# A two-layer graph kernel: attention and scores of the last batches as one block of matmuls, with bank copies and statistics moved

## Chip, cores and metric

The kernel runs on one core of a Trainium2 chip. The metric is device time in microseconds (us), the median of several runs; lower is better. Engines are named as in the profile: PE (TensorE), DVE (VectorE), ACT (ScalarE), POOL (GpSimd), and SP, which issues the DMAs.

## What is computed

There are 128 batches of a 128 x 512 matrix `x` in fp32, and one 128 x 128 matrix `adj`, which is a weight in layer 0 and the attention mask in layer 1.

```python
def layer0(x, W1, W2, b):                 # W1 = W2 = adj
    A = einsum('od,bdn->bon', W1, x)
    C = einsum('od,bdn->bon', W2, x) + b[None, :, None]
    pre = A[:, :, None, :] + (C - A)[:, :, :, None]
    return max(relu(pre), axis=-1)

def layer1(x, w_qkv, w_proj, b_proj, gamma, beta, mask):   # H = 8 heads of 64
    q, k, v = split_heads(x @ w_qkv)
    attn = einsum('bhnd,bhmd->bhnm', q, k) * scale
    attn = softmax(where(mask == 0, -inf, attn))
    o = merge_heads(attn @ v) @ w_proj + b_proj
    return o + layernorm(o) * gamma + beta

x = layernorm(x + layer0(x, adj, adj, L0_gnn_b))
x = layernorm(x + layer1(x, w_qkv, w_proj, b_proj, gamma, beta, adj))
```

Since both weights of layer 0 are the same matrix, its result is one number per row, `max(A) + b`, cut at zero.

## The kernel before

**Tiling.** Batches go through in 32 groups of four (`G = 4`). The projections of a group (queries and keys in two units, values, output) are computed with a seven-product scheme: a `Unit` stands for a matrix of 2 x 2 blocks made from seven products instead of eight. Each `product(i)` is four matmuls of 128x128 by 128x256, which the profile lists as eight, and adds into one of four PSUM banks, b1 to b4: products 1, 6 and 7 into bank 1, product 2 into bank 2, products 5 and 3 into bank 3, product 4 into bank 4. The left sides are the four blocks and four sums of blocks (s1 to s4, called `s_x` and `s_o` in the profile). Products 5, 6 and 7 use the first, second and third sum, product 3 the fourth.

**Copies of bank 1.** After product 1 (`snap(1)`), product 6 (`snap(2)`) and product 7 (`snap(3)`) ACT copies bank 1 to SBUF. `result(half, col)` on DVE adds such a copy to another bank. A product into bank 1 has to wait until the copy before it has read the bank. `relay()` copies bank 1 into bank 2 instead, so that product 2 adds onto it, and `relayed()` copies bank 2 to its place: two copies on ACT instead of a copy on ACT and a sum on DVE. `seed(unit, bank)` writes the bias into a bank before the first product into it.

**Attention.** `scores(b, banks)` makes eight small matmuls (64 rows deep) into two banks, `softmax_mask` scales and masks them on DVE, `softmax_max` takes the maxima on DVE, `softmax_exp` is eight exponentials on ACT, `prob_out` divides and transposes on DVE and writes to DRAM through SP, `prob_read` reads back, `attend` makes eight small matmuls (64 columns wide) into one bank, and `attend_copy` copies this on ACT.

**Tails.** `tail_inner` (ACT) applies the layer norm to a projected output, `tail_residual` (POOL, three steps: gamma, output, residual rows) finishes the sum, `tail_outer` (ACT) is the last norm, and a store follows. `stats` takes means and variances on DVE (`bn_stats`, `bn_aggr`) and finishes them on POOL: an addition, a power, and, for entries that are normalized on ACT, a product. With `fused=1` the first entry is normalized on DVE and leaves this product out. `fused_open`, `fused_close` (DVE) and `add_rows` (PE) do a tail in another way, `scalar_stats` takes statistics on ACT.

**Order.** Every instruction is pinned: each engine runs its own instructions in the order in which the program lists them, SP's DMAs too. A head (first eight batches of layer 0), a loop over pairs of batches, and a last part, with `L = 127` (the last batch), `LQ = 63` (the last pair) and `NG = 32`, are written out by hand. In the loop, `group_block` puts the attends of four batches and the scores of the next four directly behind each other on PE. In the last part the attends of batches 120 and 121 and the scores of 124/125 and 126/127 stand apart, with products between them. `keep_warm` multiplies zeros in the head.

[...] A new tile in a bank waits for the readers of the old one.

Of the kernel before, what the change touches and what calls it, by code (L numbers as in the profile page):

```python
# [16 lines left out]
def kernel(  # L17
# [33 lines left out]
    H = 8  # L51
    HD = D // H
    KC = D // P
    G = 4
# [250 lines left out]
    def l0_norm(f):  # L305
        normalize(xs[f], xs[f], ("y", f))

    def l0_norm_vector(f, mv):
        rs, _ = stat_of.pop(("y", f))
        pin(nc.vector.tensor_scalar(xs[f], xs[f], mv[:, 0, 0:1], rs, ALU.subtract, ALU.mult))  # L310
# [91 lines left out]
    def scores(b, banks=("pss0", "pss1")):  # L402
        g, h, jj = place(b)
        pss[b] = [
            psum.tile([P, NP, P], F32, tag=tag, name=f"pss{par}_{b}")
            for par, tag in enumerate(banks)
        ]
        for pr in range(NP):
            for par in range(2):
                t = qk[g, pr // 2, h][ds(par * HD, HD), :, pr % 2, ts(jj, P)]  # L410
                pe(pss[b][par][:, pr], lhsT=t[:, 0], rhs=t[:, 1], start=True, stop=True)

    def softmax_mask(b, order=(0, 1), place=None):

        s = place or sb.tile([P, 2, NP, P], F32, tag="s", name=f"s_{b}", bufs=4)
        for par in order:
            pin(
                nc.vector.scalar_tensor_tensor(  # L418
                    s[:, par],
                    pss[b][par],  # L420
                    SCALE,
                    mask.unsqueeze(1).to_broadcast([P, NP, P]),
                    ALU.mult,
                    ALU.add,
                )
            )
        del pss[b]
        prob[b] = s.rearrange("p a h m -> p (a h) m")

    def softmax_max(b):  # L430
        if b in pss:
            softmax_mask(b)
        nmax[b] = small.tile([P, H], F32, tag="nmax", name=f"nmax_{b}")
        pin(nc.vector.tensor_reduce(nmax[b], prob[b], AX.X, ALU.max, negate=True))  # L434

    def softmax_exp(b, heads=range(H)):
        if 0 in heads:
            psums[b] = small.tile([P, H], F32, tag="sums", name=f"sums_{b}")
        for i in heads:
            pin(  # L440
                nc.scalar.activation(  # L441
                    prob[b][:, i],
                    prob[b][:, i],
                    AF.Exp,
                    bias=nmax[b][:, i : i + 1],
                    accum_out=psums[b][:, i : i + 1],
                )
            )
# [44 lines left out]
    def attend(b, tag="po"):  # L493
        g, h, jj = place(b)
        v, t = vs[g, h], pT.pop(b)
        pos[b] = psum.tile([P, NP, P], F32, tag=tag, name=f"po_{b}")
        for pr in range(NP):
            for par in range(2):
                pe(
                    pos[b][ds(par * HD, HD), pr],  # L500
                    lhsT=v[:, jj, ds((2 * pr + par) * HD, HD)],
                    rhs=t[:, :, par * NP + pr],
                    start=True,
                    stop=True,
                )

    def attend_copy(b):
        g, h, jj = place(b)
        if jj == 0:
            tag = "x" if (g, h) == (NG - 2, 0) else "oT"  # L510
            oT[g, h] = sb.tile([P, KC, HT], F32, tag=tag, name=f"oT_{g}_{h}", bufs=2)
        pin(nc.scalar.copy(oT[g, h][:, :, ts(jj, P)], pos.pop(b)))
# [88 lines left out]
    def tail_inner(q):  # L601
        zp[q] = sb.tile([P, 2, D], F32, tag="z", name=f"z_{q}")
        for j in range(2):
            b = 2 * q + j
            normalize(zp[q][:, j], o_of(b), ("o", b))
            zs[b] = rs_[b]

    def tail_residual(q):
        z, r, (g, h) = zp.pop(q), xr.pop(q), divmod(q, 2)
        rs_pair[q] = r  # L610
        tt(nc.gpsimd, z, z, ga_bc.unsqueeze(1).to_broadcast([P, 2, D]), ALU.mult)
        tt(nc.gpsimd, z, z, os_[g, h], ALU.add)
        tt(nc.gpsimd, r, r, z, ALU.add)
# [27 lines left out]
    def tail_inner_one(b):  # L641
        z_tile(b)
        normalize(zs[b], o_of(b), ("o", b))
# [31 lines left out]
    def columns(name, *items):  # L675

        mv = small.tile([P, NC, 2], F32, tag="mv", name=f"mv_{name}")
        for k, (kind, b) in reversed(list(enumerate(items))):
            bn({"o": o_of, "z": zs.get, "y": xs.get}[kind](b), mv, k)
        return mv, items  # L680

    def stats(name, *items, fused=0):
        stat = columns(name, *items)
        finish_stats(*stat, fused)
        return stat[0]
# [40 lines left out]
        l0_add(f)  # L726
    stats("first_0", ("y", 0))
    l0_norm(0)
    mv = stats("first_1", ("y", 1), fused=1)
    weight_sums(wqk, 0, HE, 1)  # L730
    l0_max(2)
    l0_add(2)
    l0_norm_vector(1, mv)
    keep_warm(3)
    for f in range(2):
        l0_transpose_pe(f)
    l0_max(3)
    l0_add(3)
    weight_sums(wqk, 0, HE, 2)
    mv = stats("first_2", ("y", 2), ("y", 3), fused=1)  # L740
    l0_norm_vector(2, mv)
    l0_norm(3)
    weight_sums(wqk, 0, HE, 3)
    weight_sums(wqk, HE, HE)
    keep_warm(2)
# [7 lines left out]
    cur.snap(1)  # L753
    cur.product(2)
    l0_mm(4, "pa")
    for f in range(2, G):
        l0_transpose_pe(f)
    for f, tag in zip(range(5, 2 * G), ("po", "pss0", "pss1")):
        l0_mm(f, tag)
    run_sums(sums[:3], nc.vector)  # L760
    run_sums(sums[3:])
# [2 lines left out]
        l0_spill(q)  # L764
    cur.result(0, 0)
    cur.product(4)
    cur.product(5)
    cur.product(6)
    cur.snap(2)
    for f in range(G, 2 * G):  # L770
        l0_max(f)
        if f < 2 * G - 1:
            l0_add(f)
# [319 lines left out]
    second.snap(2)  # L1093
    second.product(5)
    second.result(0, 0)
    second.product(4)
    second.product(7)


    before, o_u, v_u = second, o_unit(NG - 3), v_unit(NG - 1)  # L1100
    attend(L - 7)
    before.snap(3)
    seed(o_u, 1)
    attend_copy(L - 7)
    attend(L - 6, "pa")
    attend_copy(L - 6)
    before.result(1, 1)
    before.result(1, 0)
    prob_out(L - 4)
# [3 lines left out]
    o_u.relay()  # L1113
    tail_outer(LQ - 7)
    tail_store(LQ - 7)
    tail_inner(LQ - 6)
    before.product(3)
    before.result(0, 1)
    seed(o_u, 3)
    tail_residual(LQ - 6)  # L1120
    o_u.product(2)
    o_u.relayed()
    scores(L - 3)
    scores(L - 2, po_pa)
    tail_reload(LQ - 5)
    wlast, room = last_load()
    for q in range(3):
        tail_reload_to(LQ - 2 + q, room[:, ds(2 * q, 2)])
    softmax_max(L - 3)
    softmax_max(L - 2)  # L1130
    place_of = {
        b: room[:, ds(2 * q, 2)].rearrange("p a (h m) -> p a h m", m=P)
        for b, q in ((L - 1, 3), (L, 4))
    }
    o_u.product(6)
    o_u.snap(2)
    softmax_exp(L - 3)
    o_u.product(4)
    o_u.product(5)
    o_u.product(7)  # L1140
    scores(L - 1)
    scores(L, po_pa)
    softmax_exp(L - 2, range(4))
    o_u.snap(3)
    softmax_exp(L - 2, range(4, H))
    prob_out(L - 3)
    o_u.result(1, 1)
    o_u.result(1, 0)
    softmax_mask(L - 1, place=place_of[L - 1])
    softmax_max(L - 1)  # L1150
    stats("last_1", ("o", L - 9), ("o", L - 8))
    v_u.product(1)
    v_u.relay()
    softmax_exp(L - 1, range(4))
    o_u.product(3)
    v_u.product(2)
    o_u.result(0, 1)
    prob_out(L - 2)
    softmax_exp(L - 1, range(4, H))
    v_u.relayed()  # L1160
    softmax_mask(L, place=place_of[L])
    softmax_max(L)
    for t in (L - 9, L - 8):
        tail_inner_one(t)
        tail_residual_one(t)
    v_u.product(6)
    v_u.snap(2)
    softmax_exp(L)
    v_u.product(5)
    v_u.product(7)  # L1170
    v_u.snap(3)
    v_u.product(4)
    stat = columns("last_2", ("o", L - 11), ("o", L - 10))
    prob_out(L - 1)


    o_u = o_unit(NG - 2)
    seed(o_u, 1)
    attend(L - 5)
    attend_copy(L - 5)  # L1180
    attend(L - 4, "pa")
    attend_copy(L - 4)
    prob_read(L - 3)
    prob_read(L - 2)
    v_u.result(1, 1)
    v_u.result(1, 0)
    run_sums(o_sums(NG - 2))
    o_u.lefts = o_lefts[NG - 2]
    o_u.product(1)
# [5 lines left out]
    o_u.product(2)  # L1195
    o_u.relayed()
    seed(o_u, 3)
    for t in (L - 11, L - 10):
        tail_inner_one(t)
    o_u.product(4)  # L1200
    o_u.product(6)
    o_u.snap(2)
    last_seed(L - 3, "b2")
    tail_residual_one(L - 11)
    stats("last_3", ("z", L - 13), ("z", L - 12), ("z", L - 9), ("z", L - 8))
# [51 lines left out]
    fused_close(L - 3)  # L1257
    tail_residual_one(L - 4, [0, 1])
    tail_outer_one(L - 7)
    mv = stats("last_8", ("o", L - 1), ("z", L - 6), ("z", L - 3), fused=1)  # L1260
    fused_open(L - 1, mv[:, 0, 0:1], rows=False)
    add_rows(L - 1)
    fused_close(L - 2)
    finish_scalar_stats(stat5)
    tail_residual_one(L - 4, [2])
    for t in (L - 3, L - 6, L - 5):
        tail_outer_one(t)
    stat4 = scalar_stats(L - 4)
    mv = stats("last_9", ("o", L), ("z", L - 2), fused=1)
    fused_open(L, mv[:, 0, 0:1], rows=False)  # L1270
    add_rows(L)
    fused_close(L - 1)
    tail_outer_one(L - 2)
    stats("last_10", ("z", L - 1))
    finish_scalar_stats(stat4)
    fused_close(L)
    for t in (L - 1, L - 4):
        tail_outer_one(t)
    mv = stats("last_11", ("z", L), fused=1)
    tail_outer_vector(L, mv[:, 0, 0:1])  # L1280


# [39 lines left out]
```

## Time and profile before

| | |
|---|---|
| median of 3 runs | 1933.93 us (1933.15 to 1934.26) |
| the profiled execution | 1933.73 us, its span 1931.9 us |
| busy in the span | PE 1918.5, DVE 1592.1, POOL 1290.4, ACT 1054.2 us |
| granted PE clock | 0.999 |
| head: PE's first product | starts at 14.43 us |
| last part: products of the unit `second` | start at 1841.18 us |
| last matmul on PE | starts at 1923.39 us |
| last tile finished on DVE | 1928.92 us |

The span runs from the first to the last instruction; the 1.8 us between it and the time of the same execution lie around it. "Busy" of PE includes matmuls that overlap, so that start-to-start distances are the better price of a matmul. The profile also names for each engine what ended its waits. All moments below are us from the start of the span.

### The profile page before, as it was taken

The page shows a single profiled execution, that of the slowest core. Times are in us where ns is not written, and L with a number is a line of the kernel's source. Part 1 is how long each engine was busy: PE and PEld are TensorE (multiplying, and loading weights), DVE is VectorE, ACT ScalarE, POOL GpSimd, SP SyncE. Part 2 cuts the span into 40 slices and gives each one's busy share as a digit, 9 for nine tenths or more (in the row PEclk, how much of TensorE's full clock was granted, in tenths as well). Part 3 has the DMA queues.
Part 4 walks back from the last instruction along what each step waited for, and adds up shares of the span by engine and source line. Part 5 has one row for each costly group of instructions (what it writes and reads, how often), then busy time and mean ns, then how long its engine had stood idle before and what let it go on. Part 6 is the DMA issues. An engine that isn't in the chain of part 4 may idle for free.

```text
span 1931.9 us, 33367 instructions
## 1 busy us (share of the span) xinstructions
PE 1918.5 (99%) x11541; PEld 1638.3 (85%) x11541; DVE 1592.1 (82%) x2514; ACT 1054.2 (55%) x3093; POOL 1290.4 (67%) x823
## 2 busy tenths in 40 slices
PE   9999999999999999999999999999999999999997
PEld 6888888888888888888888888888888888888885
DVE  6867888888888888888888888888888888888887
ACT  3444655645555556555465564555555555556476
POOL 6445766767667676676676676866767666667648
PEclk9999999999999999999999999999999999999999
DMA  7756676676676666766666756667666676666665
GB/s 221 175 134 152 172 189 176 171 183 159 186 202 159 186 161 180 205 161 177 171 176 188 182 167 186 153 186 207 154 186 164 183 200 164 175 178 172 164 209 162
DMA packets 444936, 341.76 MB, mean 177 GB/s; under 512 B 276832, under 2 KB 378336, under 8 KB 444768
## 3 DMA queue, kind: packets, MB, share of 16 engines
q1 hardware_dynamic: 444336, 338.85, 65.7%
q8 instruction: 91, 1.49, 0.3%
q10 hardware_dynamic: 432, 0.79, 0.1%
q14 instruction: 77, 0.63, 0.1%
HBM read 172.82 MB, written 166.72 MB: 176 GB/s over the span
## 4 chain that ended last, share of the span: by engine, by line
PE 96%; DVE 2%; POOL 1%; ACT 1%; issue 0%; POOLq 0%; ACTq 0%; DVEq 0%
PE b_qk L75 40%; PE b_v L75 19%; PE b_o L75 19%; PE pss L75 6%; PE po L75 6%; PE pa L75 6%; DVE st_mv_last L262 0%; POOL zl L78 0%; POOL s_o L78 0%; ACT s L441 0%; DVE s L78 0%; PE idle L75 0%; DVE o L78 0%; DVE mv_last L263 0%; DVE pu L462 0%
## 5 line engine op out<-in xcount | busy, mean ns | idle before, releaser
L75 PE MATMUL b_qk<-s_x,wqk 128*128 128x256 f32 x2048 | 473.1, 379 | 0.7 <-ACT u_qk L187 0.7
L75 PEld LDWEIGHTS b_qk<-s_x,wqk 128*128 128x128 f32 x2048 | 389.0, 190 | 54.5 <-ACT u_qk L187 1.1
L441 ACT ACTIVATE s<-s,nmax 128x128 f32<-128x128 f32 x1008 | 390.2, 391 | 4.5 <-DVE nmax L434 4.5
L75 PE MATMUL b_qk<-x1T,wqk 128*128 128x256 f32 x1536 | 360.5, 381 | 0.1
L276 POOL TENSOR_SCALAR rs_mv<-mv 128x6 f32<-128x6 f32 (+2 forms) x61 | 14.8, 243 | 499.9 <-DVE mv L263 499.9
L75 PEld LDWEIGHTS b_qk<-x1T,wqk 128*128 128x128 f32 x1536 | 289.3, 190 | 43.0 <-issue 1.0
L78 DVE TENSOR_TENSOR s<-s,rec 128x1024 f32<-128x1024 f32 x126 | 282.2, 2240 | 4.3
L78 DVE TENSOR_TENSOR qk<-b_qk,u_qk 128x512 f32<-128x512 f32 x256 | 170.2, 686 | 138.8 <-ACT u_qk L187 86.5
L187 ACT COPY u_qk<-b_qk 128x512 f32<-128x512 f32 x192 | 112.5, 586 | 278.2 <-PE b_qk L75 276.7
L75 PE MATMUL b_v<-wv,s_x 128*128 128x256 f32 x1024 | 237.2, 379 | 0.2
L75 PE MATMUL b_o<-wp,s_o 128*128 128x256 f32 x992 | 229.6, 379 | 0.4 <-ACT u_o L187 0.4
L418 DVE SCALAR_TENSOR_TENSOR s<-pss,mask 128x512 f32<-128x512 f32 x252 | 156.2, 681 | 78.1 <-PE pss L75 77.9
L75 PEld LDWEIGHTS b_v<-wv,s_x 128*128 128x128 f32 x1024 | 194.3, 190 | 27.4 <-DVE qk L78 0.5
L75 PEld LDWEIGHTS b_o<-wp,s_o 128*128 128x128 f32 x992 | 188.2, 190 | 26.5 <-issue 0.9
L78 POOL TENSOR_TENSOR z<-z,ga_bc 128x1024 f32<-128x1024 f32 x58 | 164.0, 2827 | 51.1 <-ACT z L285 51.1
L441 ACT ACTIVATION_READ_ACCUMULATOR s<-s,nmax 128x1 f32 x1008 | 190.8, 189 | 0.0
L78 POOL TENSOR_TENSOR x<-x,be_bc 128x1024 f32<-128x1024 f32 x64 | 178.2, 2785 | 17.5 <-DVE xt L323 16.2
L187 ACT COPY u_v<-b_v 128x512 f32<-128x512 f32 x95 | 55.6, 585 | 244.6 <-PE b_v L75 241.7
L187 ACT COPY u_o<-b_o 128x512 f32<-128x512 f32 x91 | 53.3, 586 | 248.0 <-PE b_o L75 248.0
L75 PE MATMUL b_v<-wv,x1T 128*128 128x256 f32 x768 | 176.5, 379 | 0.0
L75 PEld LDWEIGHTS b_v<-wv,x1T 128*128 128x128 f32 x768 | 145.8, 190 | 32.3 <-issue 13.9
L75 PE MATMUL b_o<-wp,oT 128*128 128x256 f32 x744 | 171.1, 379 | 0.3 <-ACT b_o L556 0.3
(135 smaller groups left out, 3309.8 us busy)
## 6 DMA issues: line engine op xcount, KB each, us to landing
hop<-pu SPq DMA_DIRECT2D x128, 512.0 KB, 3.1
pT<-hop SPq DMA_DIRECT2D x512, 128.0 KB, 3.6
spill<-x SPq DMA_DIRECT2D x64, 512.0 KB, 5.0
x<-in_x_dram SPq DMA_DIRECT2D x62, 512.0 KB, 4.3
xhop<-xt SPq DMA_DIRECT2D x248, 128.0 KB, 2.3
x1T<-xhop SPq DMA_DIRECT2D x248, 128.0 KB, 3.9
xr<-spill SPq DMA_DIRECT2D x59, 512.0 KB, 3.4
out_dram<-xr SPq DMA_DIRECT2D x58, 512.0 KB, 4.2
```

The costliest lines, as they stand in the source:

```text
L75: pin(nc.tensor.matmul(*args, **kwargs))
L78: pin(eng.tensor_tensor(dst, a, b, op))
L187: pin(nc.scalar.copy(t, self.banks[1]))
L276: pin(nc.gpsimd.tensor_scalar(rs[:, :n], mv[:, :n, 1], EPS, None, ALU.add))
L418: nc.vector.scalar_tensor_tensor(s[:, par], pss[b][par], SCALE, mask.unsqueeze(1).to_broadcast([P, NP, P]), ALU.mult, ALU.add,)
L441: nc.scalar.activation(prob[b][:, i], prob[b][:, i], AF.Exp, bias=nmax[b][:, i : i + 1], accum_out=psums[b][:, i : i + 1],)
```

## The change

In the head, batch 1 is normalized on ACT instead of DVE; of batches 2 and 3, batch 2's statistics come first on DVE, 3 is normalized on DVE and 2 on ACT, and they are transposed in the order 3, 2. In the first unit product 5 moves behind product 6 and its copy.

In the last part, product 7 of the unit `second` and its copy move ahead of product 4. The attends of batches 120 and 121 move from the front of the next stage into one block with the scores of batches 124 to 127, which use other banks (the fourth takes those of the first again); the masks follow the block in a given order. The tail of batches 114 and 115 (`LQ - 6`) and the reloads with `last_load` move behind the block. The exponentials of batches 124 to 127 are divided anew between the copies of bank 1. `v_u.relay()` and `v_u.relayed()` become `v_u.snap(1)` and `v_u.result(0, 0)`. `o_unit(NG - 2)` and its seed move ahead of the last twelve exponentials, and `v_u.result(1, 1)` and `(1, 0)` ahead of the last attends. `tail_inner_one` of batches 116 and 117 moves behind product 6 of the next unit. At the very end, statistics, outer norms and the third residual step of batch 123 change places, each of batches 125, 126 and 127 has statistics of its own, and the last norm of batch 126 goes to DVE.

```diff
     stats("first_0", ("y", 0))
     l0_norm(0)
-    mv = stats("first_1", ("y", 1), fused=1)
+    stats("first_1", ("y", 1))
+    l0_norm(1)
     weight_sums(wqk, 0, HE, 1)
     l0_max(2)
     l0_add(2)
-    l0_norm_vector(1, mv)
...
-    mv = stats("first_2", ("y", 2), ("y", 3), fused=1)
-    l0_norm_vector(2, mv)
-    l0_norm(3)
+    mv = stats("first_2", ("y", 3), ("y", 2), fused=1)
+    l0_norm_vector(3, mv)
+    l0_norm(2)
...
-    for f in range(2, G):
+    for f in (3, 2):
         l0_transpose_pe(f)
-    for f, tag in zip(range(5, 2 * G), ("po", "pss0", "pss1")):
+    for f, tag in zip(range(5, 2 * G), ("po", "pss1", "pss0")):
         l0_mm(f, tag)
...
     cur.product(4)
-    cur.product(5)
     cur.product(6)
     cur.snap(2)
+    cur.product(5)
...
     second.product(5)
     second.result(0, 0)
+    second.product(7)
+    second.snap(3)
     second.product(4)
-    second.product(7)
...
     before, o_u, v_u = second, o_unit(NG - 3), v_unit(NG - 1)
-    attend(L - 7)
-    before.snap(3)
     seed(o_u, 1)
-    attend_copy(L - 7)
-    attend(L - 6, "pa")
-    attend_copy(L - 6)
     before.result(1, 1)
...
-    tail_inner(LQ - 6)
     before.product(3)
     before.result(0, 1)
     seed(o_u, 3)
-    tail_residual(LQ - 6)
     o_u.product(2)
     o_u.relayed()
-    scores(L - 3)
-    scores(L - 2, po_pa)
+    for t, tag in zip((L - 7, L - 6), po_pa):
+        attend(t, tag)
+        attend_copy(t)
+    for t, banks in zip(
+        range(L - 3, L + 1), (("pss0", "pss1"), ("po", "b4"), ("pa", "b2"), ("pss0", "pss1"))
+    ):
+        scores(t, banks)
+    tail_inner(LQ - 6)
+    tail_residual(LQ - 6)
     tail_reload(LQ - 5)
     wlast, room = last_load()
...
-    softmax_max(L - 3)
-    softmax_max(L - 2)
...
+    softmax_mask(L - 3)
+    softmax_mask(L - 2, (1, 0))
+    softmax_max(L - 3)
+    softmax_mask(L - 1, (1, 0), place_of[L - 1])
+    softmax_mask(L, place=place_of[L])
+    softmax_max(L - 2)
     o_u.product(6)
     o_u.snap(2)
-    softmax_exp(L - 3)
-    o_u.product(4)
+    softmax_exp(L - 3, range(4))
     o_u.product(5)
     o_u.product(7)
-    scores(L - 1)
-    scores(L, po_pa)
-    softmax_exp(L - 2, range(4))
     o_u.snap(3)
-    softmax_exp(L - 2, range(4, H))
+    softmax_exp(L - 3, range(4, H))
+    o_u.result(1, 1)
+    o_u.product(4)
+    o_u.result(1, 0)
+    v_u.product(1)
+    v_u.snap(1)
+    o_u.product(3)
+    softmax_exp(L - 2)
     prob_out(L - 3)
-    o_u.result(1, 1)
-    o_u.result(1, 0)
-    softmax_mask(L - 1, place=place_of[L - 1])
+    o_u.result(0, 1)
+    v_u.product(2)
+    v_u.result(0, 0)
     softmax_max(L - 1)
     stats("last_1", ("o", L - 9), ("o", L - 8))
-    v_u.product(1)
-    v_u.relay()
+    v_u.product(6)
+    v_u.snap(2)
     softmax_exp(L - 1, range(4))
-    o_u.product(3)
-    v_u.product(2)
-    o_u.result(0, 1)
     prob_out(L - 2)
-    softmax_exp(L - 1, range(4, H))
-    v_u.relayed()
-    softmax_mask(L, place=place_of[L])
     softmax_max(L)
     for t in (L - 9, L - 8):
         tail_inner_one(t)
         tail_residual_one(t)
-    v_u.product(6)
-    v_u.snap(2)
-    softmax_exp(L)
     v_u.product(5)
     v_u.product(7)
     v_u.snap(3)
+    o_u = o_unit(NG - 2)
+    seed(o_u, 1)
+    softmax_exp(L - 1, range(4, H))
+    softmax_exp(L)
     v_u.product(4)
+    v_u.result(1, 1)
+    v_u.result(1, 0)
     stat = columns("last_2", ("o", L - 11), ("o", L - 10))
     prob_out(L - 1)
-    o_u = o_unit(NG - 2)
-    seed(o_u, 1)
...
-    v_u.result(1, 1)
-    v_u.result(1, 0)
...
     seed(o_u, 3)
-    for t in (L - 11, L - 10):
-        tail_inner_one(t)
     o_u.product(4)
     o_u.product(6)
     o_u.snap(2)
+    for t in (L - 11, L - 10):
+        tail_inner_one(t)
...
     tail_outer_one(L - 7)
+    finish_scalar_stats(stat5)
+    tail_outer_one(L - 5)
     mv = stats("last_8", ("o", L - 1), ("z", L - 6), ("z", L - 3), fused=1)
...
     fused_close(L - 2)
-    finish_scalar_stats(stat5)
-    tail_residual_one(L - 4, [2])
-    for t in (L - 3, L - 6, L - 5):
+    for t in (L - 3, L - 6):
         tail_outer_one(t)
-    stat4 = scalar_stats(L - 4)
-    mv = stats("last_9", ("o", L), ("z", L - 2), fused=1)
+    mv = stats("last_9", ("o", L), fused=1)
     fused_open(L, mv[:, 0, 0:1], rows=False)
     add_rows(L)
     fused_close(L - 1)
+    tail_residual_one(L - 4, [2])
+    stat4 = scalar_stats(L - 4)
+    stats("last_10", ("z", L - 2))
     tail_outer_one(L - 2)
-    stats("last_10", ("z", L - 1))
+    fused_close(L)
+    mv = stats("last_11", ("z", L), fused=1)
     finish_scalar_stats(stat4)
-    fused_close(L)
-    for t in (L - 1, L - 4):
-        tail_outer_one(t)
-    mv = stats("last_11", ("z", L), fused=1)
+    tail_outer_one(L - 4)
+    mv1 = stats("last_12", ("z", L - 1), fused=1)
     tail_outer_vector(L, mv[:, 0, 0:1])
+    tail_outer_vector(L - 1, mv1[:, 0, 0:1])
```

## The prediction

> **What bounds the kernel now.** I read four views. The page first: PE is busy 1918.5 of 1931.9 us, and the chain that ended last is nearly all PE.
>
> ```profile
> PE 96%; DVE 2%; POOL 1%; ACT 1%; issue 0%; POOLq 0%; ACTq 0%; DVEq 0%
> ```
>
> So only PE's own time counts up to about 1900, and PE's waits (second view: us in total, times, longest) say what was lost:
>
> ```profile
> PE pp L75 <- DVE z L654: 1.5, 1, 1.5
> PE pt L333 <- DVE x L310: 0.7, 2, 0.4
> PE b_qk L75 <- ACT u_qk L187: 0.7, 1, 0.7
> PE b_o L75 <- ACT u_o L187: 0.4, 1, 0.4
> PE b_o L75 <- ACT b_o L556: 0.3, 1, 0.3
> ```
>
> The third view, PE's timeline of the last part, gives prices (start, duration):
>
> ```profile
> 1767.13 3.84 PE L75 MATMUL pss<-qk 64*128 64x128 f32 x64
> 1770.90 1.99 PE L75 MATMUL b_qk<-x1T,wqk 128*128 128x256 f32 x8
> ...
> 1853.45 1.97 PE L75 MATMUL po<-pT,v 128*64 128x128 f32 x32
> 1855.35 1.99 PE L75 MATMUL b_o<-wp,oT 128*128 128x256 f32 x8
> ...
> 1860.72 2.06 PE L75 MATMUL pss<-qk 64*128 64x128 f32 x32
> 1862.71 1.99 PE L75 MATMUL b_o<-wp,s_o 128*128 128x256 f32 x8
> ...
> 1869.81 2.06 PE L75 MATMUL pss<-qk 64*128 64x128 f32 x32
> ```
>
> A product (8 matmuls) is 1.73 from start to start and 1.83 after another kind of matmul. Past 1900, DVE is dense in the chain and POOL nearly so. The fourth view, the timelines of ACT, DVE and POOL, shows what the moved steps wait for:
>
> ```profile
> 1849.97 0.57 ACT L187 COPY u_qk<-b_qk 128x512 f32<-128x512 f32 x1
> ...
> 1885.42 0.56 ACT L187 COPY u_v<-b_v 128x512 f32<-128x512 f32 x1
> 1886.02 0.59 ACT L556 COPY b_o<-bp_bc 128x512 f32<-128x512 f32 x1
> ```
>
> ```profile
> 1889.64 2.14 POOL L78 TENSOR_TENSOR s_o<-s_o,oT 128x512 f32<-128x512 f32 x1
> 1891.74 1.27 POOL L78 TENSOR_TENSOR s_o<-oT,oT 128x512 f32<-128x512 f32 x1
> ```
>
> [...] v_u.product(7) ended at 1882.5, but its copy (snap 3) began at 1885.42, behind eight exponentials that ended at 1885.33, and cost PE 0.33. [...] The trace shows it as the 0.7 wait for u_qk: product 7 writes bank 1 and waits until snap 2 has read it. [...] the POOL sum at 1889.64 takes 2.14 instead of 1.27 beside the DVE division of 1888.53, itself 2.12 instead of 1.23.
>
> **Part 1, the head.** Normalizing batch 1 on DVE took 1.48 (11.31 to 12.80). On ACT it needs one more POOL multiply (0.2, after the power ended at 11.28) and 0.81: done at 12.4, 0.4 earlier. This passes through transposes, DVE copies and l0_max(3) to l0_add(3), which ends at 15.5 instead of 15.9. Statistics of batch 2 now precede those of batch 3 and fill DVE's wait for l0_add(3); only batch 3's remain behind it, 0.79 less. From its aggregate (16.4 instead of 17.6), batch 3 is normalized on DVE 1.7 later (18.1; 19.33 before), batch 2 on ACT 2.2 later (18.65; 19.86 before). PE ends products 1, 2 and l0_mm(4) at 18.5 and transposes 3, then 2 without a wait: 1.19, to 19.7 instead of 20.57. That is 0.9. Then l0_mm(5) to (7), product 4, and 6 before 5: snap 2 runs under product 5, and the 0.7 stall at 29.00 goes. Product 6 wants sum s1 at 23.8; DVE ends it at about 23.0. **Head: −1.6**, between −1.0 (part of the 0.9 caught by a DVE-POOL collision) and −1.8. Nothing between 29 and 1840 takes it back: PE has no wait there, and DVE, ACT and POOL are driven by it (POOL waits 3.7 at 36.2).
>
> **Part 2, PE up to 1889** (times of the old clock, without the head).
> - Three blocks of small matmuls become one. Old: 0.09 in + 1.90 + 0.10 out, then twice 0.09 + 1.99 + 0.10, together 6.45. New: attends and four scores as in the loop, 0.09 + 1.9 + 3.77 + 0.10 = 5.86. **−0.6.** The fourth scores reuse pss0 and pss1 at 1864.1; DVE has read them (mask of batch 124, 1862.5 to 1863.8), 0.3 to spare.
> - second.product(7) now follows 5 instead of 4. It wants bank 1 at 1849.86; snap 2 ends at 1850.54, behind the exponentials of batch 123 in ACT's queue. **+0.7.** snap 3 and seed then lie under product 4.
> - snap 3 and seed of the next unit come before twelve exponentials: the 0.33 stall goes. **−0.3.**
>
> - At nothing: tail_inner and tail_residual of 114/115 move behind the block (ACT 1.5 from 1861.9, POOL 3 × 2.4 to 1870.6); POOL's old idle of 8.4 before 1876.5 covers them. Masks and maxima of the last four batches run on DVE from 1862.5 to 1869.8 and free b4 and b2 first, seconds before products 4 and v_u.2 ask; seed(o_u, 3) ends at 1859.7, relayed at 1860.25, ahead of the second attend copy (1862.0).
>
> PE is then where it was: v_u.product(2) ends at 1877.3 (1877.1 before).
>
> **Part 3, what gets late.** DVE now takes result(0,0) of v_u (0.68, not before 1877.3) ahead of softmax_max(L−1) (1.22) and the statistics last_1: they begin at 1879.1, not 1874.72. **+4.4** on everything behind them:
> - ACT's tail_inner of batches 118/119 starts at 1883.1 (1878.67 before) and ends at 1884.5. snap 3 and seed end at 1885.5, twelve exponentials of 0.385 at 1890.1, two attend copies at 1891.1, o_u.relay at 1891.6. PE wants o_u.product(2) at 1889.7. The cover is gone: **+1.9** (1.2 if POOL's last small multiply is not shut out, 2.5 if its power is too).
> - POOL's six residual steps and then the sums s_o start 4.4 late: s1 ends at 1896.2 (1891.78 before). PE reaches product 6 at 1891.65 + 1.83 + 1.73 = 1895.2: **+1.0** (0 to 1.5).
> - The old 0.39 before product 7 goes, since tail_inner of 116/117 is now behind snap 2: **−0.4.** Product 7 starts at 1896.2 + 3.56 = 1899.8, old 1897.68: +2.1. This is the sum of parts 2 and 3 (2.3) within rounding.
> - SP: the wlast load and reloads, now behind the block, have no reader for 30 us. The write of batch 126's probabilities waits for a transpose ending about 1891; eight reads behind it issue in 4.1 and land near 1899, wanted at 1901.6. Hidden, barely.
>
> **Part 4, the end.** ACT's tail_inner of 116/117 waits for POOL (s3 ends 1898.6, statistics 1.3 more), runs to 1901.4, the seed of bank b2 to 1901.9; o_u.snap(3) ends at 1902.5 and DVE's results start 2.2 late. POOL is 4.4 late and stays dense: it loses its idle (0.6 + 0.3, and gaps of some 0.7) and gains one statistics chain with two fewer columns elsewhere (+0.4, from rs 0.23 + power 0.57). Its last power, now for batch 126 or 127, ends 4.4 − 1.6 + 0.4 = 3.2 after 1928.34; tensor_scalar (0.55) and the store follow as before. Batch 126's last step is 0.55 on DVE instead of 0.81 on ACT, and the closing of batch 127 moves ahead; both only matter if POOL is in time. The wait of the last add_rows (1.5) stays hidden beside this. **Last part: +3.2**, from +0.5 (no shut-out, POOL regains more idle) to +5.
>
> **Sum.** −1.6 + 3.2 = +1.6 on the profiled execution: 1933.73 (span 1931.9 and 1.8 around it) becomes 1935.3. The median of the runs, 1933.93, lies 0.2 above: **1935.5**. A measurement tells about 0.2% (3.9 us) from no change, so this is "same", on the slow side.
>
> **Rivals.**
> - *A, the forecast:* chance 0.6, own range 1934 to 1937.
> - *B, covered anyway:* the exponentials and s_o come early enough, PE keeps −1.6 −0.6 +0.7 −0.3 −0.4 = −2.2, and the reordered end, where batch 127 no longer queues behind others' statistics, up to 1.5 more: 1930.2 to 1931.8. For it: ACT is idle 1.4 to 3.6 at a time between 1863 and 1883 in the new order. Against: that idle lies ahead of the exponentials in program order. Chance 0.2, a quarter of it past −3.9.
> - *C, slower:* POOL becomes the bound of the whole end. It has no idle from 1884 on, so each further shut-out by a DVE instruction adds its 0.87. Three more than before give +1.6 + 2.6 = 4.2: 1938.1; with two it still counts as same. For: two struck among POOL's ten steps from 1879.56 to 1894.24. [...] Chance 0.16.
> - *D, not done as said:* scores of batch 127 wait for the mask of batch 124 because DVE is behind, and the block breaks; +0.5 on A: 1936. Chance 0.04.
>
> **Numbers.** A, D and three quarters of B are within 0.2%: 0.79; C slower: 0.16; the rest of B faster: 0.05. The range leaves out C's far end and most of B's gain: 1931.8 to 1938.2.
>
> **What would show it.** Product 7 of the first unit near 27.4 with no wait for u_qk there, but one of 0.7 near 1849; po x32 directly followed by pss x64 in the last part; PE waits of 1 to 2.5 on the relay copy (ACT) and up to 1.5 on s_o (POOL) near 1890; last_1 some 4 late; POOL without idle at the end. I am wrong if PE shows no wait at 1886 to 1897, if the head gains under 1, or if the stretch behind PE's last matmul grows by over 3.

## The result, and the profile after

The changed kernel takes 1936.97 us (median of 20 runs, 1936.62 to 1937.64) beside 1933.55 for the kernel before on the same chip: ratio 1.0017 [1.0011, 1.0024], **3.4 us slower**, and within the 0.2% that the prediction called "same". The profiled execution took 1936.71, its span 1934.9.

The page of the changed kernel looks as before. In the chain that ended last, one per cent has gone over from DVE to POOL:

```profile
PE 96%; POOL 2%; DVE 1%; ACT 1%; DMA 0%; issue 0%; POOLq 0%; SPq 0%; ACTq 0%; DVEq 0%
```

PE's waits (us in total, times, longest) are the ones that were forecast: the two of the head that the prediction names (0.7 and 0.7) are gone, one of 0.5 for `u_qk` has come near 1848, and two have come near 1890:

```profile
PE b_o L75 <- ACT b_o L192: 2.3, 1, 2.3
...
PE pp L75 <- DVE z L654: 0.9, 1, 0.9
PE b_o L75 <- POOL s_o L78: 0.8, 1, 0.8
...
PE b_qk L75 <- ACT u_qk L187: 0.5, 1, 0.5
```

PE's timeline shows the same in place (start, duration; in brackets the wait and who ended it). First comes product 7 of `second`, then the block with a further product before it. Then come the two late groups of `o_u` (products 2 and 4; 6, 5 and 7), and then the last matmuls:

```profile
1848.18 1.99 PE L75 MATMUL b_qk<-s_x,wqk 128*128 128x256 f32 x8 [0.53 <-ACT u_qk L187]
...
1855.20 1.89 PE L75 MATMUL b_o<-wp,oT 128*128 128x256 f32 x8
1857.02 1.97 PE L75 MATMUL po<-pT,v 128*64 128x128 f32 x32
1858.91 3.84 PE L75 MATMUL pss<-qk 64*128 64x128 f32 x64
1862.68 5.45 PE L75 MATMUL b_o<-wp,s_o 128*128 128x256 f32 x24
...
1889.77 3.72 PE L75 MATMUL b_o<-wp,oT 128*128 128x256 f32 x16 [2.28 <-ACT b_o L192]
1894.29 5.45 PE L75 MATMUL b_o<-wp,s_o 128*128 128x256 f32 x24 [0.80 <-POOL s_o L78]
...
1922.90 1.12 PE L75 MATMUL pp<-wlast,ident 128*128 128x512 f32 x2 [0.93 <-DVE z L654]
```

Here one sees why the waits are not the whole answer. PE's last matmuls start at 1922.90, 0.5 *earlier* than before (1923.39), and yet the span is 3.0 longer. The stretch behind PE has grown, from 7.4 (1924.5 to 1931.9) to 10.9 (1924.0 to 1934.9). POOL and DVE work there. POOL's timeline has the statistics of batches 118 and 119, their residual steps at `zl`, then the sums:

```profile
1878.66 0.23 POOL L276 TENSOR_SCALAR rs_mv_last<-mv_last 128x2 f32<-128x2 f32 x1 [10.31 <-DVE mv_last L263]
1878.98 1.73 POOL L78 TENSOR_TENSOR rs_mv_last<-rs_mv_last,mhalf 128x2 f32<-128x2 f32 x1
...
1881.91 1.28 POOL L78 TENSOR_TENSOR zl<-zl,ga_bc 128x512 f32<-128x512 f32 x1 [0.93 <-ACT zl L285]
...
1890.64 2.25 POOL L78 TENSOR_TENSOR s_o<-oT 128x512 f32<-128x512 f32 x1
```

The same places in the kernel before:

```profile
1876.51 0.23 POOL L276 TENSOR_SCALAR rs_mv_last<-mv_last 128x2 f32<-128x2 f32 x1 [8.36 <-DVE mv_last L263]
...
1879.56 1.27 POOL L78 TENSOR_TENSOR zl<-zl,ga_bc 128x512 f32<-128x512 f32 x1 [0.93 <-ACT zl L285]
```

The first `zl` step starts at 1881.91 (1879.56 before): 2.35 later on the clock, although PE had come 2.4 earlier to `second` (1838.77 instead of 1841.18). POOL stood idle for 10.31 ahead of its statistics, because DVE was late with them; from 1898.9 it has no idle over 0.2. The last sum ends at 1896.7 (1894.24), and POOL's last power at 1930.66 (1928.34). The lateness looks as if it went through unchanged (2.35, 2.46, 2.32), but e7_old_end below shows two terms in the last figure: with the old end it is 1.56, and the new end adds 0.77. DVE's timeline ends so:

```profile
1928.48 0.55 DVE L689 TENSOR_SCALAR z<-z,mv_last,rs_mv_last 128x512 f32<-128x512 f32 x1 [0.28 <-POOL rs_mv_last L78]
1930.70 0.55 DVE L689 TENSOR_SCALAR z<-z,mv_last,rs_mv_last 128x512 f32<-128x512 f32 x1 [1.67 <-POOL rs_mv_last L78]
```

In the kernel before it ended so:

```profile
1928.37 0.55 DVE L689 TENSOR_SCALAR z<-z,mv_last,rs_mv_last 128x512 f32<-128x512 f32 x1 [1.53 <-POOL rs_mv_last L78]
```

That is 2.33 of the 3.0. The other 0.67 lies behind DVE: from the end of its last instruction to the end of the span it was 2.98 and is 3.65. The changed kernel's stores at the end, from SP's timeline:

```profile
1930.58 0.33 SPq L673 DMA_DIRECT2D out_dram<-zl  x1
1931.00 0.87 SPq L690 DMA_DIRECT2D out_dram<-z  x2
```

Three stores of 256 KB (batches 123, 127, 126) are issued within 1.3 us. Before, the one of batch 123 was followed by one more:

```profile
1928.25 0.33 SPq L673 DMA_DIRECT2D out_dram<-zl  x1
1928.95 0.33 SPq L690 DMA_DIRECT2D out_dram<-z  x1
```

In the changed kernel batch 127 was ready at 1929.03, but its store is queued on SP behind that of batch 123. What the DMA engines moved in the window 1928 to 1938, in slices of 0.25 us, in the changed kernel:

```profile
GB/s 0 0 0 0 0 0 139 360 385 164 0 0 0 123 369 393 361 393 385 385 393 336 8 0 0 0 0 0 0 0 0 0 0 0 0 0 0 0 0 0
```

and in the kernel before:

```profile
GB/s 377 393 115 0 246 369 377 361 385 344 17 0 0 0 0 0 0 0 0 0 0 0 0 0 0 0 0 0 0 0 0 0 0 0 0 0 0 0 0 0
```

The last train is about 2.1 us long at some 385 GB/s (three stores) instead of 1.5 (two), and the store of the last tile, batch 126, is the last one issued. A store of 256 KB at 385 GB/s is some 0.68 us of such a train (an estimate from these two figures).

### The profile page after: what moved, and what is told of

Same layout as the page of the kernel before. It is cut to its first block, busy times and chain, and to the rows that moved or that the text cites. A ratio compares the mean times of both kernels' runs of the same rounds, so it can differ in the third digit from the quotient of the medians.

```text
span 1934.9 us, 33376 instructions
## 1 busy us (share of the span) xinstructions
PE 1916.9 (99%) x11541; PEld 1638.2 (85%) x11541; DVE 1590.6 (82%) x2515; ACT 1054.4 (54%) x3092; POOL 1290.9 (67%) x825
## 4 chain that ended last, share of the span: by engine, by line
PE 96%; POOL 2%; DVE 1%; ACT 1%; DMA 0%; issue 0%; POOLq 0%; SPq 0%; ACTq 0%; DVEq 0%
PE b_qk L75 40%; PE b_v L75 19%; PE b_o L75 19%; PE pss L75 6%; PE po L75 6%; PE pa L75 6%; POOL zl L78 1%; POOL rs_mv_last L78 0%; DMA x<-in_x_dram 0%; POOL s_o L78 0%; ACT zl L285 0%; ACT s L441 0%; DVE s L78 0%; PE idle L75 0%; DVE st_mv_last L262 0%
```

## Experiments

The theories: **P**, the tail of batches 118 and 119 comes late to POOL, which then sets the end; **Q**, PE's own waits of 2.3 and 0.8 near 1890 set it; **R**, the new order at the very end costs by itself. All differences are to the kernel before, measured on the same chip; the changed kernel itself stands at +3.4.

| run | median (runs), us | ratio to before | difference |
|---|---|---|---|
| e1_head | 1931.59 (13) | 0.9989 [0.9981, 0.9997] | −2.1 |
| e2_last | 1938.97 (7) | 1.0028 [1.0017, 1.0039] | +5.3 |
| e3_stats_early | 1935.02 (13) | 1.0008 [1.0000, 1.0016] | +1.3 |
| e4_exp_late | 1937.85 (13) | 1.0022 [1.0013, 1.0030] | +4.2 |
| e5_cut_after | 1935.66 (21) | 1.0012 [1.0006, 1.0019] | +2.0 |
| e6_cut_before | 1933.49 (13) | 0.9998 [0.9990, 1.0007] | −0.1 |
| e7_old_end | 1935.59 (21) | 1.0010 [1.0003, 1.0016] | +2.0 |
| e8_tail_early | 1933.41 (13) | 0.9999 [0.9991, 1.0007] | −0.2 |
| e9_early_old_end | 1932.44 (13) | 0.9992 [0.9984, 1.0000] | −1.5 |
| e10_all | 1931.63 (21) | 0.9989 [0.9982, 0.9995] | −2.3 |
| e11_warm | 1937.47 (13) | 1.0019 [1.0011, 1.0027] | +3.6 |
| e12_dve_add | 1931.10 (21) | 0.9987 [0.9981, 0.9994] | −2.4 |

The intervals reach 1.2 to 2.1 us to either side. Where two variants differ by less than that, the text says what else tells them apart: ranges of runs that don't overlap, or the traces. The profiled executions of kernels with the new head also differ by up to 0.9 in when PE's first product starts (13.66 in the changed kernel, 14.53 in e5_cut_after), before any edit of the last part can act.

**Each half alone.** e1_head has the head of the changed kernel (up to product 5 behind product 6) and the last part of before; e2_last the reverse.

> Only the head of the change (up to the loop); the last part is that of before. The trace of after is 2.4 us ahead of that of before when the last part begins. Theory P and Q alike (the loss lies in the last part alone): the head is worth 1.6 (as predicted) to 2.4 us and keeps it to the end, 1933.55 - 2.4 = 1931.2. Rival H (the head's lead is a chance of the first loads, or is caught again by the end): 1933 to 1933.6.

> Only the last part of the change; head as before. Theory P and Q: the two parts add, 1936.97 + 2.4 = 1939.4, between 1938.6 and 1939.6. Rival H (head's lead not kept): 1937.

−2.1 and +5.3 make +3.2, the whole +3.4 within the intervals: the halves add up. In e1_head PE's last matmuls start at 1921.11 and DVE's last instruction at 1926.07, each 2.3 before those of the kernel before (1923.39 and 1928.37). The head's gain arrives at the end with either last part; so the last part has to be explained by itself.

**P against Q.** e3_stats_early lets DVE take the statistics before it waits for PE:

```diff
     o_u.product(4)
     o_u.result(1, 0)
+    stats("last_1", ("o", L - 9), ("o", L - 8))
     v_u.product(1)
...
     softmax_max(L - 1)
-    stats("last_1", ("o", L - 9), ("o", L - 8))
```

e4_exp_late leaves them and takes the relay copy out from behind the exponentials:

```diff
     softmax_exp(L - 1, range(4, H))
-    softmax_exp(L)
...
     o_u.product(1)
     o_u.relay()
+    softmax_exp(L)
```

> After, with the statistics last_1 taken directly behind o_u.result(1, 0), ahead of the probabilities of batch 124, v_u.result(0, 0) and the maxima of batch 126. Theory P (late last_1 makes ACT's tail_inner of batches 118/119, hence POOL's residual steps and all POOL work to the end late): ACT starts that tail behind the four exponentials of batch 126, at about 1879.2 instead of 1881.0; POOL and the end come 1.8 earlier: 1935.1; the wait of product 2 shrinks from 2.3 to about 0.5. Theory Q (PE's waits set the loss) expects about the same, 1935. Rival R (the loss comes from the reordered last steps after PE's end): no change, 1937.0.

> After, with the eight exponentials of batch 127 moved behind the two attend copies and o_u.relay on ACT. Theory P (POOL bounds the end, PE's wait for the relay costs nothing by itself): PE's wait of 2.3 for the relay goes, its wait for the sum s1 grows from 0.8 to about 3, and the time moves by less than 0.4: 1936.6 to 1937.3. Theory Q (ACT's backlog in front of the relay, by PE's wait of 2.3, is what costs): 1936.97 - 2.3 = 1934.7.

e3_stats_early gained 2.1, its slowest run (1935.70) lying below the changed kernel's fastest (1936.62). On its PE the relay wait is nearly gone:

```profile
1887.98 3.72 PE L75 MATMUL b_o<-wp,oT 128*128 128x256 f32 x16 [0.31 <-ACT b_o L192]
1892.53 5.45 PE L75 MATMUL b_o<-wp,s_o 128*128 128x256 f32 x24 [0.83 <-POOL s_o L78]
```

e4_exp_late took the same wait away from PE altogether, and gained nothing (+4.2 instead of +3.4). PE merely waited at the next place, for POOL:

```profile
1895.01 8.40 PE L75 MATMUL b_o<-wp,s_o 128*128 128x256 f32 x24 [3.37 <-POOL s_o L78]
```

The same three products took 5.45 in the changed kernel and 8.40 here. The stretches of e4_exp_late (window, its length, busy time and number of instructions of PE, PEld, DVE, ACT and POOL, then the granted PE clock, the DMA share and GB/s) show the clock halved, 0.50, after the pause. (This execution was the slowest of its 13 runs, 1939.22; the others go down to 1936.50.)

```profile
1895.00:1898.00 3.00, 2.99 (x7) 2.45 (x8) 2.60 (x8) 0.00 (x0) 2.92 (x4) 0.50 1.10 252
1898.00:1901.00 3.00, 3.00 (x8) 2.37 (x8) 0.00 (x0) 2.17 (x4) 1.40 (x3) 0.50 1.06 271
```

So it could not yet be said whether Q fell or only paid for the clock. e11_warm is e4_exp_late with the pause filled:

```diff
     o_u.product(4)
+    fill = psum.tile([P, 2 * P], F32, tag="po", name="fill")
+    for _ in range(7):
+        pe(fill, lhsT=zeros[:, :P], rhs=zeros, start=True, stop=True)
     o_u.product(6)
```

> e4_exp_late with seven multiplications of zeros (0.43 each) on PE in the wait before product 6. In e4 PE waited 3.4 there, and the three products after it took 8.4 instead of 5.4 at a granted clock of 0.50. If the pause itself is what lowers the clock: no pause over 1, the products take 5.4, the time is 1936.5 to 1937.0 (e4: 1937.85, from 1936.5). If the clock falls for another reason (DMA or power of the other engines): 8.4 as in e4, 1937.8.

```profile
1891.46 3.19 PE L75 MATMUL fill<-zeros 128*128 128x256 f32 x14
1894.98 5.45 PE L75 MATMUL b_o<-wp,s_o 128*128 128x256 f32 x24 [0.34 <-POOL s_o L78]
```

The products are back at 5.45 and the clock at 1.00, but the time, 1937.47, is only some 0.6 below e4_exp_late, above the expected 1936.5 to 1937.0, and as long as the changed kernel's. In this profiled execution PE's first product starts 0.67 later than in that of the changed kernel (14.33 instead of 13.66), long before the edit; product 6 starts 0.69 later (1894.98 instead of 1894.29) and DVE's last instruction 0.68 later (1931.38 instead of 1930.70). The edit itself moved neither. With no relay wait and no slow clock nothing is won, because product 6 has to wait for POOL's sum in either order. So Q falls for the relay: that wait is a sign of the late tail, not the loss. The run does not bring PE to product 6 any earlier, so whether PE's lateness there costs something has to be asked in another way.

**Who is the bound.** In e5_cut_after and e6_cut_before the multiplication by gamma is left out of the residual step of batches 116 and 117 (two POOL steps of 1.27), in the changed kernel and in the one before:

```diff
-    tail_residual_one(L - 11)
+    tail_residual_one(L - 11, [1, 2])
...
-    tail_residual_one(L - 10)
+    tail_residual_one(L - 10, [1, 2])
```

> After, but POOL leaves out the multiplication by gamma for batches 116 and 117, two of its instructions (1.35 from start to start) that come after the last sum that PE waits for. PE's waits stay as in after (2.3 and 0.8). Theory P (POOL's queue bounds the end): the end comes by up to 2.7 earlier, 1934.3; less if DVE takes over as the bound, but at least 1.5 earlier. Theory Q (PE's waits set the end): no change, 1937.0.

> Before, with the same two multiplications by gamma left out. Theory P: before the change DVE's chain and not POOL's queue bounded the end, so at most 0.5 is gained: 1933.2 to 1933.7. If POOL bounded the end there too, 2.7 are gained: 1931.

Before, 2.5 of POOL's work less is worth nothing (−0.1); after, 1.4, just short of the 1.5 that was the least expected. The cut lies behind the last sum that PE waits for, so PE's waits have no reason to change (the one for the relay is 2.28 in the profile of e5_cut_after as well). So POOL has become a bound, though less than the 2.5 came through. In the profiled execution of e5_cut_after a slower PE stepped in: after the same pause of 2.28 its two products took 5.41 instead of 3.72, at a lower clock. PE's timeline and, below it, the stretches of e5_cut_after (averages of the clock; if it changed between 1.00 and 0.50 alone, they put 0.50 from 1891.4 to 1894.8, an estimate):

```profile
1890.64 5.41 PE L75 MATMUL b_o<-wp,oT 128*128 128x256 f32 x16 [2.28 <-ACT b_o L192]
```

```profile
1890.60:1893.30 2.70, 2.66 (x8) 2.21 (x9) 2.67 (x2) 0.00 (x0) 2.70 (x2) 0.64 0.75 257
1893.30:1896.00 2.70, 2.70 (x11) 2.23 (x10) 2.63 (x6) 1.23 (x3) 2.62 (x3) 0.73 0.92 223
```

The times of its 21 runs lie in two heaps, 1935.2 to 1936.2 and 1936.5 to 1937.1. The mean granted clock of the whole execution is 0.998 in 14 of the 15 lower runs and 0.997 in five of the six upper ones, which fits a slow stretch like this one. It isn't shown to be the only reason: the profiled run is of the upper heap, and its first product also started 0.87 later than the changed kernel's. The lower heap alone has its median at 1935.57.

**The end (R).** e7_old_end is the changed kernel with the statements from `tail_outer_one(L - 7)` to the end in the order of before.

> After, with the order of the last steps (from the closing of batch 124 on) as before: two batches in one chain of statistics, the last norm of batch 126 on ACT. Theory P: POOL is late either way; the old order saves one POOL chain (0.4) and the new one lets batch 127 pass: 1936.5 to 1937.5. Rival R (the new order is the loss): 1935 or less.

It gained 1.4, to +2.0, its slowest run (1936.22) below the changed kernel's fastest (1936.62). DVE's last instruction starts at 1929.93 instead of 1930.70 (0.77), and from its end to that of the span 3.02 pass instead of 3.65 (0.63). R is right in part: 1.4 of the 3.4, and 2.0 that come from elsewhere.

**Undoing P.** e8_tail_early is e3_stats_early with the tail itself moved on ACT and POOL:

```diff
     softmax_exp(L - 2)
+    for t in (L - 9, L - 8):
+        tail_inner_one(t)
+        tail_residual_one(t)
     prob_out(L - 3)
...
     softmax_max(L)
-    for t in (L - 9, L - 8):
-        tail_inner_one(t)
-        tail_residual_one(t)
```

> After, with last_1 directly behind o_u.result(1, 0) and the tail of batches 118/119 (ACT and POOL) behind the exponentials of batch 125, ahead of those of 126. Theory P: ACT starts that tail at about 1875.2, POOL at 1876 instead of 1881.9; its six steps end before the attend copies are there, the sums s_o start at about 1887.3 (1890.6 in after), PE has no wait there of over 0.5, and the end comes 3 to 4.5 earlier: 1932.5 to 1934. Rival R (order of the last steps): not below 1935, since the earlier start is lost there.

It brings −3.6 against the changed kernel, and ends level with the kernel before. POOL's first `zl` step of e8_tail_early is 5.4 earlier than in the changed kernel (3.0 earlier than before), its sums now wait for the attend copies and not for POOL itself, and near 1890 PE waits 0.16 for the relay and 0.32 for a seed where it had waited 2.28 and 0.80:

```profile
1876.52 1.28 POOL L78 TENSOR_TENSOR zl<-zl,ga_bc 128x512 f32<-128x512 f32 x1 [1.33 <-ACT zl L285]
...
1887.65 1.27 POOL L78 TENSOR_TENSOR s_o<-oT 128x512 f32<-128x512 f32 x1 [2.35 <-ACT oT L512]
```

The late tail is worth 3.6 of the last part's 5.3. The early tail took PE's waits away as well, so this run alone doesn't say through which of the two engines the gain came; with e5_cut_after, where PE's waits stay and 1.4 is gained on POOL alone, P holds for at least that much. e9_early_old_end adds the old end to this:

> The two repairs together: the early tail of batches 118/119 (gain of 3.6 alone) and the old order of the last steps (gain of 1.4 alone). Theory P with the order of the last steps as a loss of its own (one POOL chain more, and three stores close together at the end): the two add, 1936.97 - 3.6 - 1.4 = 1932.0. If the order of the last steps only costs where POOL is late: 1933.0 to 1933.5.

It gave −1.3 more, near the −1.4 of e7_old_end: the two costs add up and are separate.

**Going on.** e10_all is e9_early_old_end with two further moves, one against the wait of product 7, one to free the results of `v_u` from `prob_out`:

```diff
-    softmax_exp(L - 4)
+    softmax_exp(L - 4, range(6))
     prob_out(L - 5)
...
     second.snap(2)
+    softmax_exp(L - 4, range(6, H))
     second.product(5)
...
-    prob_out(L)
     v_u.result(0, 1)
+    prob_out(L)
```

> e9_early_old_end, with two exponentials of batch 123 behind snap 2 (so that product 7 of the unit second doesn't wait 0.5 for it) and v_u.result(0, 1) ahead of the probabilities of batch 127 (so that seed 3 comes in time, 0.3). If PE bounds the last part again, 0.8 less than e9: 1931.2, below the head alone (1931.6). If DVE's or POOL's queue bounds it: as e9, 1932.

That brought 0.8 (1931.63 beside 1932.44 on one chip; the ranges of the runs overlap in part) and PE's wait of 0.5 is gone. At −2.3 it does no better than the head alone (−2.1). PE's last matmuls begin at 1919.30, 1.8 earlier than in e1_head (1921.11), but DVE's last instruction begins at 1926.12, no earlier (1926.07). DVE's timeline of e10_all says what took PE's lead:

```profile
1922.58 0.75 DVE L663 SCALAR_TENSOR_TENSOR z<-z,rs_mv_last,pp 128x512 f32<-128x512 f32 x1 [1.48 <-POOL rs_mv_last L78]
```

There DVE waits for POOL, as it does for its last instruction. e12_dve_add takes one addition from POOL:

```diff
-    tail_residual_one(L - 4, [2])
...
-    stat4 = scalar_stats(L - 4)
...
     add_rows(L)
+    tt(nc.vector, zs[L - 4], zs[L - 4], rs_[L - 4], ALU.add)
+    stat4 = scalar_stats(L - 4)
```

> e10_all, with the third residual step of batch 123 (1.27 on POOL, ahead of the statistics that DVE waits 1.48 for) done on DVE (0.68) in that wait. Theory P (POOL's queue still bounds the end of e10): statistics of batch 127 come 1.3 earlier and the end about 1 earlier: 1930.6, better than the head alone. If DVE's own chain is the bound by then: 1931.6 or, by the added 0.68, 1932.3.

The wait of 1.48 is gone, and DVE's last instruction begins at 1925.49, 0.6 earlier, though it still waits 1.89 for POOL. In time it is −2.4 beside e10_all's −2.3, with intervals that overlap nearly whole: the forecast of about 1 was missed, and on top of e10_all a gain is not shown. So that POOL's queue still bounds the end of e10_all is seen in the trace and not confirmed by the time. Both beat the kernel before and the changed one.

## Why the prediction was right, and which terms were off

The verdict ("same, on the slow side") and the mechanism of rival A were right, and the time of 1936.97 is inside its range and inside A's own. The sum was +1.6 instead of +3.4: two errors of opposite sign, −0.5 in the head and +2.1 in the last part. That the sum held is in part luck: each part lies just outside its own range (the head beyond −1.8, the last part beyond +5), on opposite sides, and 1936.97 is only 0.03 below the top of A's range.

- **Part 1, the head, −1.6.** Measured −2.1 (e1_head). All steps went as written: the transposes at 18.05 follow without a wait, product 4 starts at 21.51 (22.98 before), the wait of product 7 is gone. The lead at `second` was 2.4 in this trace. 0.25 of that is there already at the second pair of first-layer matmuls (8.09 instead of 8.34), and differs from run to run (7.88 in e3_stats_early, 8.51 in e11_warm). The term too small was the first one: 0.9 up to the end of the transposes, where product 4 came 1.47 earlier, or 1.2 without the 0.25. The first product started at 13.66, 0.77 earlier, since PE's own wait of 0.36 between the first transposes is gone, where 0.4 was passed on; the second 0.7, for product 7, was as forecast.
- **Part 2, PE up to 1889.** The block takes 5.85, counted as in the forecast with the 0.09 and 0.10 at its edges (1856.93 to 1862.78), forecast 5.86. Product 7 waited 0.53 instead of 0.7. The old wait of 0.3 for a seed is not there. The right size to 0.2.
- **Part 3, what gets late.** "+4.4 on everything behind them" was right: statistics at 1876.88 instead of 1874.72 while PE is 2.2 to 2.4 early. The wait for the relay was 2.28 (1.9, range 1.2 to 2.5), that for s1 0.80 (1.0). The power took 1.73 instead of 0.71 beside a DVE division, but before, the small multiply behind it had taken 1.02 instead of 0.20, so that this nearly cancelled (1.93 and 1.73 for the two).
- **Part 4, the end, +3.2: the failed term.** It was to hold 4.4 − 1.6 + 0.4. Measured: +5.3 (e2_last). Two sentences in it were wrong, and one size. One, "tensor_scalar (0.55) and the store follow as before": with three stores behind each other the last arrives 0.67 later, and the sum had no term for it. Two, the reorder at "+0.4" for one statistics chain more: POOL's last power is 0.77 later for it. Together the new end costs 1.3 to 1.4 (e7_old_end, and e9_early_old_end beside e8_tail_early) where 0.4 stood. The size: 1.6 of the 4.4 was taken off for idle that POOL would use up; the tail alone costs 3.6 (e8_tail_early), so about 0.8 was regained. The trace of e7_old_end agrees: POOL is 2.47 late after its sums and 1.56 late at its last power, 0.9 less, about the two idles of 0.58 and 0.30 that it had before. The gaps of some 0.7 gave nothing back.
- **PE and POOL.** The working let the waits of part 3 and the lateness of part 4 stand beside each other and priced the end by POOL. That was right as far as it was tested: when the cause of the longer wait was taken away (e4_exp_late, e11_warm), PE waited for POOL instead and the end stayed, and POOL's work behind PE's waits is worth 1.4 by itself (e5_cut_after).
- **Rivals.** B (covered anyway) falls by the waits on PE. C was right that POOL becomes the bound (e5_cut_after beside e6_cut_before), but its mechanism, three further shut-outs (POOL steps drawn out beside a DVE instruction, like the sum of 2.14 instead of 1.27 at 1889.64 before), did not happen: POOL is busy 1290.9 us in all, 1290.4 before, and between 1876 and 1897 two of its steps take over 2.1 in either kernel (2.13 and 2.25; 2.14 and 2.14 before). D did not happen. Of "I am wrong if", one point came true: the stretch behind PE's last matmul grew by 3.5, over 3. It was the right alarm, for the term that was too small.

Left open: whether `relay` to `snap` and `result(0, 0)`, taken alone, makes the lateness (only the place of the statistics and of the tail were tried), and why the rest of the change of the last part, as left in e10_all, is worth no more than −0.2 although the block is 0.6 shorter. DVE's waits for POOL, seen there, suggest a reason, but taking 1.27 of work from POOL (e12_dve_add) changed the time by no more than 0.1.

## What to carry to other kernels

When a queue's order is changed, follow what the *other* engines of the last stage receive: a wait for a product (1.10) and two DVE steps (0.69 and 1.21), put in front of statistics on DVE, went with a rise of POOL's idle from 8.4 to 10.3 us. The late tail came back as 3.6 us at the end, while PE's timeline showed it only as two short waits. A PE wait that only turns into a wait for another engine when its cause is taken away is a symptom; look for the engine that has no idle from there to the end. And price the last stores together: with three of them issued within 1.3 us, 3.65 us passed here between the end of DVE's last instruction and that of the span, with two 2.98.

## What the runs showed of the hardware

- **A pause of PE that cost more than itself.** In the pause of 3.37 us of e4_exp_late the granted clock fell to 0.50, 2.6 us after the pause began; it stayed there for some 6.8 us (1894.2 to 1901.0), and three products took 8.40 instead of 5.45. With the pause filled with multiplications of zeros the clock stayed at 1.00 and the products took 5.45 (e11_warm). After a pause of 2.28 us in the profile of the changed kernel the clock was 1.00 (1889.7 to 1896.0), and two products took 3.72; in that of e7_old_end they took 3.72 after 2.28 as well. In that of e5_cut_after the same pause of 2.28 was followed by 0.50 for some 3.4 us (1891.4 to 1894.8), which began 0.7 us after PE had resumed, and two products took 5.41 instead of 3.72. (These moments are estimates from averages of the clock, if it changed between 1.00 and 0.50 alone: in e4_exp_late 0.89 in 1891.5 to 1895.0, 0.50 in both stretches up to 1901.0 and 0.99 in 1901.0 to 1904.0; in e5_cut_after the two stretches shown above.) That the pause is the cause in e5_cut_after is the author's estimate and not tested. How long a pause has to be was not shown: of three profiles with 2.28 us, one had the lower clock behind it.
- **Three stores at the end took longer than two.** From the end of DVE's last instruction to the end of the span, 3.65 to 3.69 us pass in all seven profiles in which three stores of 256 KB are issued at the end within 1.3 us (the changed kernel and e2, e3, e4, e5, e8, e11), and 2.98 to 3.06 us in all seven with two (before and e1, e6, e7, e9, e10, e12).
